# Layer 0's experts on one Trainium2 core: turning routes and vectors apart, and a new order for the opening and the rows

## The chip, the core and the metric

The kernel runs on one core of a Trainium2 chip (trn2). The metric is the device time of one execution in microseconds (us). The engines are PE (TensorE; its weight loads are shown as PEld), DVE (VectorE), ACT (ScalarE), POOL (GpSimd) and SP (SyncE, which here only issues transfers). "Line 1522" or "L1522" is a line of the kernel before; where a line of the changed kernel is meant, the text says so.

## What is computed

The reference is a stack of four layers, each a cross-attention and a feed-forward part with a layernorm ahead of both, on x of shape (4, 256, 256), four batches of 256 tokens, and a context of (4, 512, 128). Only layer 0 is touched. Its attention has 16 heads of 16 channels, with normed queries and keys, and its feed-forward part routes each token to 4 of 64 "arrows" (experts) of rank 16:

```python
vecs = jnp.einsum('arh,bsh->bsar', A, x)          # 64 arrows x 16 numbers for each token
arrows = jnp.linalg.norm(vecs, axis=-1)
_, idx = jax.lax.top_k(arrows, 4)
routes = jax.nn.one_hot(idx, 64).sum(-2) / 4      # 1/4 at the four chosen, else 0
v = jnp.einsum('bsa,bsar->bsr', routes, vecs)     # 16 numbers for each token
delta = jnp.einsum('bsa,ajr,bsr->bsj', routes, B, v)
return jnp.einsum('bsh,jh->bsj', x, W) + bias + delta
```

So `delta` is a product of u = routes x v, 64 x 16 = 1024 numbers for each token, with B as a matrix of 1024 x 256.

## The kernel before

All of layer 0 is written in an order fixed by hand for PE, ACT, DVE and POOL: each engine executes its instructions in the order in which the code records them, and waits at the head of its queue. SP's order is left to a scheduler. The code has these parts, in time:

- **The opening** (to about 21 us): loads, then for batch 0 the layernorm, queries, keys and values. `warm(n)` (line 1465) does n matmuls of the identity with itself, whose result nobody reads. `rows_of_biases` lets POOL build three selecting rows; `spread_biases` (line 1188) has PE spread three bias rows over 128 partitions and ACT copy them to `bqk`, which DVE then adds to queries (line 1219) and keys (line 1235). `ones_of_values` is a series of small POOL operations, `root_aside` (lines 1293 to 1296) a POOL root for the queries' norm.
- **The attention**, batch by batch, 8 steps a batch (4 groups of heads x 2 halves of the keys). In step i of batch b, PE does scores (line 1401), ACT their exponential (1405), PE the values of the group before (1411, 1420), DVE that group's `quotient`. `between(b, i)` (line 1613) fills in other work at each step: the next batch's preparation, `output0` of the batch before, and in the last batch's steps the norms (`Norm`, `layernorm_T`) of the experts' rows and the first chunk's `vectors` and `routes`.
- **The experts' stage** (137.5 to 220.5 us): 8 chunks of 128 tokens, two for each batch, one object of class `Arrows` (line 1471) each. Its methods: `vectors`: PE multiplies tokens with A (4 matmuls of 512 columns, line 1485), ACT writes squares and copies into a tile `two` (lines 1493, 1494). `routes`: DVE alone sums squares (1502), takes the best four (1504 to 1509), multiplies (1511) and sums to v (1513); then POOL makes u = route x v (1514), tokens on the partitions. `turned`: PE turns u in eight transposes of 128 x 128 (1522), ACT copies them to `uT` (1525). `output`: PE multiplies tokens with W (1531), adds `uT` times B (1535, 16 records), DVE adds the bias (1537), POOL adds to x (1538).
- Beside the chunks, **`folding`** (line 1003) is a generator that prepares layer 1: each step is 8 records on PE (1014), two more (1030), ACT and DVE copies. Its raw weights come over SP (`load_raw`, line 998). The loop at the end of the stage interleaves these by tables of counts; each chunk's `routes` stands two chunks ahead of its `turned`.

`layernorm_T` (line 939) turns a batch's tokens by four transposes on PE and one ACT copy. `layernorm_aside` (line 969) does the same with two DVE transposes of 32 x 32 blocks and sixteen small transfers on SP's queue. `Norm` needs a root on POOL (line 928) in the middle.

Of the kernel before, what the change touches and what calls it, by code (L numbers as in the profile page):

```python
# [17 lines left out]
P = 128  # L18
# [818 lines left out]
def bounded_path(ctx: ExitStack, tc: tile.TileContext, t, out: bass.AP, over):  # L837
# [34 lines left out]
    def load_c(b):  # L872
        (nc.sync if b else nc.scalar).dma_start(c_sb[:, b], t["ctx"][b].rearrange("(k p) c -> p k c", p=P))
# [181 lines left out]
    with tc.manual_schedule(engines={E.PE, E.Activation, E.DVE, E.Pool}):  # L1055
        c0 = ExitStack()
        l0 = c0.enter_context(tc.tile_pool(name="l0", bufs=1, side="right"))

        load_x(0)
        load_c(0)  # L1060
# [3 lines left out]
        wkv = l0.tile([P, 2, 2 * D], F32, tag="wkv", name="wkv")  # L1064
        nc.scalar.dma_start(wkv[:, 0, :], t["L0_wkv"])
# [3 lines left out]
        nc.scalar.preload_act_table_set("natural_log_exp_and_others")  # L1069

# [4 lines left out]
        rows1 = w0.tile([3, D + 3 * P], F32, tag="oT0", name="rows1")  # L1075
        crow = rows1[:, :D].rearrange("n (o d) -> n o d", o=1)
        takes = rows1[:, D:].rearrange("n (i p) -> n i p", p=P)


        brow = l0.tile([1, 2, 2 * D], F32, tag="brow", name="brow")  # L1080
        nc.sync.dma_start(crow[0:1, 0, :], t["L0_bq"].partition_broadcast(1))
        for i, n in enumerate(("L0_bkv", "L0_bdca")):
            nc.sync.dma_start(
                crow[1 + i : 2 + i, 0, :].rearrange("o (h x) -> o h x", x=HD0),
                t[n].rearrange("(o h x) -> o h x", o=1, x=2 * HD0)[:, :, :HD0],
            )
# [16 lines left out]
        wb = load_fw("wb", [P, 8, D], lambda w: [(w, t["F0_bT"].rearrange("(k p) n -> p k n", p=P))], "wb", f0w)  # L1103
# [10 lines left out]
        for i, n in enumerate(("qn", "kn", "knd")):  # L1114
            nc.gpsimd.dma_start(prm[:, i], t[f"L0_{n}"].partition_broadcast(P))
# [15 lines left out]
        nc.gpsimd.memset(c_last, 0.0)  # L1131
# [56 lines left out]
        def spread_biases():  # L1188
            pb = bank("mm", [P, 2, D], "pbias0")
            for i in range(2):  # L1190
                nc.tensor.matmul(pb[:, i, :], lhsT=takes[:, i, :], rhs=crow[:, 0, :], start=True, stop=True)
            pl = bank("mm", [P, D], "pbias1")
            nc.tensor.matmul(pl, lhsT=takes[:, 2, :], rhs=crow[:, 0, :], start=True, stop=True)
            nc.scalar.copy(bqk[:, 0:2, :], pb)
            nc.scalar.copy(bqk[:, 2, :], pl)
# [111 lines left out]
        def columns_of_norms():  # L1307
            wide = [P, 3, 2, HD0]
            by_lane = l0.tile(wide, F32, tag="by_lane", name="by_lane")
            pairs = l0.tile([P, 3, 2], F32, tag="pairs", name="pairs")  # L1310
            nc.vector.tensor_tensor(by_lane, prm, lane0[:, 0, None, None, :].to_broadcast(wide), ALU.mult)
            nc.vector.tensor_reduce(pairs, by_lane, AX.X, ALU.add)
            for o in range(2):
                nc.vector.tensor_scalar(
                    cols[:, o, :], pairs[:, 0, :], halves0[:, o : o + 1], HD0 ** -0.5, ALU.mult, ALU.mult
                )
            nc.vector.tensor_copy(cols[:, 2:, :], pairs[:, 1:, :])
# [152 lines left out]

        class Arrows:
# [24 lines left out]
            def routes(self):  # L1496
# [11 lines left out]
                route = small.tile([P, NA], F32, tag="route", name=f"route{u}")  # L1508
                nc.vector.tensor_scalar(route, rest[:, :NA], 0.0, 1.0 / TOPA, ALU.is_lt, ALU.mult)
                route_b = route[:, :, None].to_broadcast([P, NA, RA])  # L1510
                nc.vector.tensor_tensor(ar, ar, route_b, ALU.mult)
                v = small.tile([P, RA], F32, tag="v", name=f"v{u}")
                nc.vector.tensor_reduce(v, ar.rearrange("p a r -> p r a"), AX.X, ALU.add)
                nc.gpsimd.tensor_tensor(sq, route_b, v[:, None, :].to_broadcast([P, NA, RA]), ALU.mult)

            def turned(self):
                self.uT = w0.tile([P, 8, P], F32, tag="qT0", name=f"uT{self.u}")
                for n in range(2):
                    pt = bank("t", [P, 4, P], f"puT{self.u}_{n}")
                    for k in range(4):  # L1520
                        a0 = 8 * (4 * n + k)
                        nc.tensor.transpose(  # L1522
                            pt[:, k, :], self.two[:, 1, a0 : a0 + 8, :].rearrange("p a r -> p (a r)"), ident
                        )
                    nc.scalar.copy(self.uT[:, 4 * n : 4 * n + 4, :], pt)
# [15 lines left out]
        warm(9)  # L1541
        context_T(0)
        norm = Norm(0, "a0_0")
        rows_of_biases()
        last_context(0)
        mq = head_sums(by_head(wq0))
        xn = norm.tokens()
        warm(3)
        xnTs[0] = layernorm_T(xn, "a0_0")
        centred(by_head(wq0), by_head(wq0), mq)  # L1550
        centred(by_head(crow), by_head(crow), head_sums(by_head(crow), 3), 3)
# [6 lines left out]
        columns_of_norms()  # L1558
        warm(3)
        add_q = project_q(0)  # L1560
        spread_biases()
        add_q()
# [49 lines left out]

        def between(b, i):

            n = b + 1
            if n == 1:
# [76 lines left out]
            if b == B - 1:  # L1693
                if i in (0, 2, 6):
                    norms["f", i // 2] = Norm(min(i // 2, 2), f"f0_{min(i // 2, 2)}")
                if i in (1, 3, 7):
                    xns["f", i // 2] = norms["f", i // 2].tokens()
                if i in (3, 5):
                    k = (i - 3) // 2
                    xnTs["f", k] = layernorm_T(xns["f", k], f"f0_{k}")  # L1700
                if i == 4:
                    arrows[0] = Arrows(0)
                    arrows[0].vectors()
                if i == 5:
                    arrows[0].routes()
# [25 lines left out]
        arrows[1].routes()  # L1731
        arrows[0].turned()
        arrows[0].output()
        output0(B - 1)
# [14 lines left out]
        for n in range(B * NC):  # L1749
            if n + 2 < B * NC:  # L1750
                arrows[n + 2].routes()
            if n:
                arrows[n].turned()
            if n % NC == 0:
                if n + 3 < B * NC:
                    arrows[n + 3] = Arrows(n + 3)
                    arrows[n + 3].vectors()
                for _ in range((0, 0, 1, 1, 2, 2, 1, 1)[n]):
                    next(fold)
                if n == 6:  # L1760
                    xn1 = norm.tokens()
                if n:
                    arrows[n].output()
            else:
                k = n // NC + 2
                if k < B:
                    xnTs["f", k] = layernorm_T(xns["f", k + (k == 2)], f"f0_{k}")
                if n == 7:
                    first_xnT = layernorm_T(xn1, "a1_0")
                    next(fold)  # L1770
# [1709 lines left out]
```

## Time and profile before

| what | us |
|---|---|
| median of 3 runs | 1380.93 (1380.93 to 1382.0) |
| the profiled execution | 1380.97 |
| its span, first to last instruction | 1379.2 |
| first scores of batch 0 | 21.03 |
| last attention matmul of layer 0 ends | 137.46 |
| layer 1's first matmul starts | 220.46 |
| mean granted clock of TensorE | 0.999 |

The page gives the busy time of each engine, then the chain of work that ended last: followed back from the last instruction, at each step to what released it. Each row of the chain is a start, a length, an engine, a tile and a line; the number after x counts records (a matmul of this kernel leaves two, a transpose one), so rows are compared by their length. In the order of time, a bracket at a row's end gives how long the engine was idle before it and who released it. A busy PE in this profile is not PE at its peak, since matmuls' ends are modelled; what counts for the bound is whether one piece begins where the last ended.

In the stage from 137.46 to 168.40 DVE was busy 27.56 of 30.94 us, in 168.40 to 193.10 it was 18.92 of 24.70, and in 193.10 to 220.50 it was 11.51 of 27.40. PE has no idle time in any of the three.

### The profile page before, as it was taken

The page shows a single profiled execution, that of the slowest core. Times are in us where ns is not written, and L with a number is a line of the kernel's source. Part 1 is how long each engine was busy: PE and PEld are TensorE (multiplying, and loading weights), DVE is VectorE, ACT ScalarE, POOL GpSimd, SP SyncE. Part 2 cuts the span into 40 slices and gives each one's busy share as a digit, 9 for nine tenths or more (in the row PEclk, how much of TensorE's full clock was granted, in tenths as well). Part 3 has the DMA queues.
Part 4 walks back from the last instruction along what each step waited for, and adds up shares of the span by engine and source line. Part 5 has one row for each costly group of instructions (what it writes and reads, how often), then busy time and mean ns, then how long its engine had stood idle before and what let it go on. Part 6 is the DMA issues. An engine that isn't in the chain of part 4 may idle for free.

```text
span 1379.2 us, 20227 instructions
## 1 busy us (share of the span) xinstructions
PE 1369.2 (99%) x7221; PEld 903.1 (65%) x7221; DVE 897.2 (65%) x2052; ACT 572.6 (42%) x1134; POOL 699.4 (51%) x848
## 2 busy tenths in 40 slices
PE   9999999999999999999999999999999999999997
PEld 7665676566656667887565666666975665666666
DVE  6767863666666557655676756558656758566675
ACT  5766454433343332256434333333364334333331
POOL 5223333566565445352577655566325676444660
PEclk9999999999999999999999999999999999999999
DMA  5000220300000001361120000000432000000001
GB/s 171 15 3 2 77 78 17 89 19 8 16 5 19 0 13 43 83 218 48 47 54 15 17 0 16 0 1 16 124 119 69 7 12 4 1 8 1 0 1 34
DMA packets 77907, 50.79 MB, mean 37 GB/s; under 512 B 40628, under 2 KB 72645, under 8 KB 77799
## 3 DMA queue, kind: packets, MB, share of 16 engines
q1 hardware_dynamic: 72262, 36.13, 9.6%
q0 software_dynamic: 4176, 12.24, 3.1%
q8 instruction: 59, 0.97, 0.3%
q10 hardware_dynamic: 1360, 1.05, 0.2%
q14 instruction: 50, 0.40, 0.1%
HBM read 38.78 MB, written 6.95 MB: 33 GB/s over the span
## 4 chain that ended last, share of the span: by engine, by line
PE 97%; POOL 2%; DVE 1%; issue 0%; ACT 0%; POOLq 0%; DVEq 0%
PE ps L1948 23%; PE po L1956 23%; PE paq L1918 6%; PE pao L1918 5%; PE pbq L1918 4%; PE pbo L1918 4%; PE ps L1401 3%; PE po L1411 2%; PE pyf L1535 2%; PE paf L1485 2%; PE pgu L2496 2%; PE pm L1014 2%; PE psh L2317 2%; PE py L2042 2%; PE pn L1030 1%; PE pb L2901 1%
## 5 line engine op out<-in xcount | busy, mean ns | idle before, releaser
L1967 POOL TENSOR_TENSOR half<-pT 128x1024 f32<-128x1024 f32 x93 | 218.4, 2349 | 282.8 <-ACT pT L1951 228.0
L1948 PE MATMUL ps<-qT,cT 128*128 128x512 f32 x768 | 345.6, 593 | 0.0
L1956 PE MATMUL po<-pT,c_sb 128*128 128x512 f32 x768 | 345.3, 592 | 0.0
L1951 ACT ACTIVATE pT<-ps,mbias 128x512 f32<-128x512 f32 x384 | 263.8, 687 | 164.0 <-PE ps L1948 147.3
L1956 PEld LDWEIGHTS po<-pT,c_sb 128*128 128x128 f32 x768 | 145.8, 190 | 183.2 <-issue 183.2
L1948 PEld LDWEIGHTS ps<-qT,cT 128*128 128x128 f32 x768 | 138.9, 190 | 138.4 <-issue 136.1
L1960 ACT COPY oT<-po 128x512 f32<-128x512 f32 x96 | 56.2, 586 | 265.2 <-PE po L1956 265.2
L2003 POOL TENSOR_TENSOR oT<-oT,wide 128x512 f32<-128x512 f32 x84 | 106.8, 1291 | 0.0
L1928 DVE TENSOR_TENSOR qT<-qT,paq 128x128 f32<-128x128 f32 x90 | 25.2, 280 | 87.1 <-ACT qT L1927 87.1
L1405 ACT ACTIVATE pT<-ps 128x512 f32<-128x512 f32 x128 | 66.0, 602 | 21.6 <-PE ps L1401 21.4
L1975 DVE TENSOR_TENSOR half<-half 128x512 f32<-128x512 f32 x96 | 71.9, 749 | 2.7 <-POOL half L1965 2.5
L1977 DVE STREAM_TRANSPOSE turned<-half 128x512 f32<-128x512 f32 x96 | 68.3, 711 | 6.3
L1918 PE MATMUL paq<-xnT_a,m_sb 128*128 128x128 f32 x360 | 71.3, 280 | 0.0
L1928 DVE TENSOR_TENSOR w<-w,pao 128x128 f32<-128x128 f32 x21 | 6.0, 285 | 99.2 <-ACT w L1927 99.2
L1918 PE MATMUL paq<-xx,m_x 128*128 128x128 f32 x360 | 69.6, 275 | 0.0
L1918 PEld LDWEIGHTS paq<-xnT_a,m_sb 128*128 128x128 f32 x360 | 57.5, 192 | 18.2 <-issue 9.2
L1981 DVE TENSOR_REDUCE sums<-turned 128x16 f32<-128x512 f32 x96 | 65.9, 686 | 3.3
L1918 PE MATMUL pao<-n_x,ox 128*128 128x128 f32 x336 | 65.0, 275 | 0.0
L1927 ACT COPY qT<-paq 128x128 f32<-128x128 f32 x90 | 23.9, 265 | 94.2 <-PE paq L1918 93.2
L1931 DVE TENSOR_TENSOR qT<-qT,pbq 128x384 f32<-128x384 f32 x90 | 49.8, 554 | 9.4
L1918 PEld LDWEIGHTS paq<-xx,m_x 128*128 128x128 f32 x360 | 54.7, 192 | 0.0
L2002 DVE STREAM_TRANSPOSE wide<-rz 128x512 f32<-128x512 f32 x84 | 54.4, 686 | 0.0
(504 smaller groups left out, 2553.9 us busy)
## 6 DMA issues: line engine op xcount, KB each, us to landing
wq<-in_L_wqT SPq DMA_DIRECT2D x8, 512.0 KB
wo<-in_L_wo SPq DMA_DIRECT2D x8, 512.0 KB
yd<-yr SPq DMA_DIRECT2D x20, 128.0 KB
xnT_a<-y_a SPq DMA_DIRECT2D x144, 16.0 KB
xd<-xn_f SPq DMA_DIRECT2D x8, 256.0 KB
w<-in_F_w SPq DMA_DIRECT2D x4, 512.0 KB
wq<-in_L_wqT POOLq DMA_DIRECT2D x3, 512.0 KB
wo<-in_L_wo POOLq DMA_DIRECT2D x3, 512.0 KB
```

Source lines behind the costliest of these rows:

```text
L1405: nc.scalar.activation(pT[kp][:, j], ps[j], AF.Exp)
L1918: nc.tensor.matmul(p[:, at, :], lhsT=lhsT, rhs=rhs, start=(k == 0 and at == 0), stop=(k == len(of) - 1 and i == which[-1]),)
L1948: nc.tensor.matmul(ps, lhsT=cT[:, b, k * P : (k + 1) * P], rhs=qT, start=True, stop=True)
L1951: nc.scalar.activation(pT[:, k, :], ps, AF.Exp, bias=mbias[:, b, k : k + 1])
L1956: nc.tensor.matmul(po, lhsT=c_sb[:, b, k, :], rhs=pT[:, k], start=(k == 0), stop=(k == NK - 1))
L1960: done["head"] = nc.scalar.copy(raw, po).ins
L1967: nc.gpsimd.tensor_tensor(half, pT[:, 0:2], pT[:, 2:4], ALU.add)
L1975: nc.vector.tensor_tensor(part, half[:, 0], half[:, 1], ALU.add)
L1977: nc.vector.transpose(turned.rearrange("p f i -> p (f i)"), part)
L1981: nc.vector.tensor_reduce(sums[b, hp // 4][:, hp % 4, :], turned, AX.X, ALU.add)
L2002: nc.vector.transpose(wide, rzs[b, hp // 4][:, hp % 4, :, None].to_broadcast([P, NB, 32]))
L2003: eng.tensor_tensor(outs[b, hp], outs[b, hp], wide.rearrange("p f i -> p (f i)"), ALU.mult)
```

## The change

**The experts.** `routes` no longer makes u on POOL. It writes the routes twice side by side (64 + 64 columns) and keeps v. `turned` turns routes (128 x 128) and v (128 x 16) by one PE transpose each, writes the turned v to a scratch in DRAM (8 KB, issued by ACT), and loads it back by two transfers on SP's queue, each of 64 partitions, in which a row of v is repeated for all arrows (256 KB each). A new method `spread` multiplies this by the turned routes on POOL, in place; `uT` now lives in the tile `two`, which is held until `output`. The rows of B are loaded in another order to match (two transfers, 8 KB rows).

**Rows.** The tokens of batches 0, 1 and 2 for the experts are turned by `layernorm_aside`, batch 0's during the attention of batch 2, the others in the last batch's. Chunk 0 has `vectors` at step 2 of the last batch instead of 4, `routes` at 3 instead of 5, and now `turned` at 5 and `spread` at 6.

**The stage's order** is written out. `routes` of chunks 5, 6 and 7 come later than before against the outputs: that of chunk 7 is between `output(5)` and one step of the fold, followed by `turned(7)`. The norm of layer 1's first rows comes ahead of `output(6)`.

**The opening.** The bias rows are loaded first, on ACT's queue; context 0 moves from ACT's queue to SP's; three small parameter loads move from POOL's queue to ACT's; the biases are spread ahead of tokens, context and queries; the `warm` matmuls of its first part go from 9, 3 and 3 to 10.

The core of the diff:

```diff
@@ opening, loads
         load_x(0)
-        load_c(0)
-        wq0 = l0.tile([P, ND, D], F32, tag="wq0", name="wq0")
-        nc.sync.dma_start(wq0, t["L0_wq"].rearrange("(d p) n -> p d n", p=P))
...
-        nc.sync.dma_start(crow[0:1, 0, :], t["L0_bq"].partition_broadcast(1))
+        nc.scalar.dma_start(crow[0:1, 0, :], t["L0_bq"].partition_broadcast(1))
...
+        wkv = l0.tile([P, 2, 2 * D], F32, tag="wkv", name="wkv")
+        load_c(0)
+        nc.scalar.dma_start(wkv[:, 0, :], t["L0_wkv"])
+        nc.scalar.dma_start(wkv[:, 1, :], t["L0_wdca"])
...
+        for i, n in enumerate(("qn", "kn", "knd")):
+            nc.scalar.dma_start(prm[:, i], t[f"L0_{n}"].partition_broadcast(P))
@@ class Arrows, routes
-                nc.gpsimd.tensor_tensor(sq, route_b, v[:, None, :].to_broadcast([P, NA, RA]), ALU.mult)
+                self.route = sq.rearrange("p a r -> p (a r)")[:, : 2 * NA].rearrange("p (h a) -> p h a", h=2)
+                nc.vector.tensor_scalar(
+                    self.route, rest[:, None, :NA].to_broadcast([P, 2, NA]), 0.0, 1.0 / TOPA, ALU.is_lt, ALU.mult
+                )
+                nc.vector.tensor_tensor(ar, ar, self.route[:, 0, :, None].to_broadcast([P, NA, RA]), ALU.mult)
+                self.v = small.tile([P, RA], F32, tag="v", name=f"v{u}")
+                nc.vector.tensor_reduce(self.v, ar.rearrange("p a r -> p r a"), AX.X, ALU.add)
             def turned(self):
-                self.uT = w0.tile([P, 8, P], F32, tag="qT0", name=f"uT{self.u}")
-                for n in range(2):
-                    pt = bank("t", [P, 4, P], f"puT{self.u}_{n}")
-                    for k in range(4):
...
-                    nc.scalar.copy(self.uT[:, 4 * n : 4 * n + 4, :], pt)
+                two = self.two.rearrange("p n a r -> p n (a r)")
+                self.routeT, vT = two[:, 0, :P], two[:RA, 0, P : 2 * P]
+                self.uT = two[:, 1].rearrange("p (k s) -> p k s", s=P)
+                pt = bank("t", [P, 2, P], f"prT{self.u}")
+                nc.tensor.transpose(pt[:RA, 1, :], self.v, ident)
+                nc.tensor.transpose(pt[:, 0, :], self.route.rearrange("p h a -> p (h a)"), ident)
+                nc.scalar.copy(vT, pt[:RA, 1, :])
+                put = turned_v[:, (self.b * NC + self.c) * P : (self.b * NC + self.c + 1) * P]
+                nc.scalar.dma_start(put, vT)
+                nc.scalar.copy(self.routeT, pt[:, 0, :])
+                for h in range(2):
+                    nc.sync.dma_start(
+                        self.uT[64 * h : 64 * h + 64],
+                        put[8 * h : 8 * h + 8].rearrange("(o k) s -> o k s", o=1).to_broadcast([64, 8, P]),
+                    )
+            def spread(self):
+                nc.gpsimd.tensor_tensor(
+                    self.uT, self.uT, self.routeT[:, None, :].to_broadcast([P, 8, P]), ALU.mult
+                )
@@ opening, order
-        warm(9)
+        warm(10)
+        rows_of_biases()
+        norm = Norm(0, "a0_0")
+        nc.gpsimd.memset(c_last, 0.0)
+        centred(by_head(crow), by_head(crow), head_sums(by_head(crow), 3), 3)
+        spread_biases(0, 2)()
+        xn = norm.tokens()
+        xnTs[0] = layernorm_T(xn, "a0_0")
+        bias_last = spread_biases(2, 3)
         context_T(0)
...
         last_context(0)
...
@@ between(b, i)
+            if b == B - 2:
+                if i == 2:
+                    norms["f"] = Norm(0, "f0_0")
+                elif i == 3:
+                    rows_of_arrows(0)
...
+                if i in (0, 6):
+                    norms["f"] = Norm(1 + i // 6, f"f0_{1 + i // 6}")
+                if i in (1, 7):
+                    rows_of_arrows(1 + i // 6)
+                if i == 2:
                     arrows[0] = Arrows(0)
                     arrows[0].vectors()
+                if i == 3:
+                    arrows[0].routes()
                 if i == 5:
-                    arrows[0].routes()
+                    arrows[0].turned()
+                if i == 6:
+                    arrows[0].spread()
@@ the stage (after the last attention)
         for n in (1, 2):
             arrows[n] = Arrows(n)
             arrows[n].vectors()
-        arrows[1].routes()
-        arrows[0].turned()
+            arrows[n].routes()
         arrows[0].output()
+        arrows[1].turned()
         output0(B - 1)
...
+        def output(n):
+            arrows[n].spread()
+            arrows[n].output()
...
+        vectors(3)
+        norm = Norm(3, "f0_3")
+        vectors(4)
+        arrows[3].routes()
+        xn3 = norm.tokens()
+        arrows[2].turned()
+        output(1)
+        next(fold)
+        arrows[3].turned()
+        arrows[4].routes()
+        vectors(5)
+        output(2)
+        context_squares(0)
+        arrows[4].turned()
+        next(fold)
+        xnTs["f", 3] = layernorm_T(xn3, "f0_3")
+        arrows[5].routes()
+        output(3)
+        context_squares(1)
+        vectors(6)
+        arrows[5].turned()
+        next(fold)
+        output(4)
+        context_squares(2)
+        vectors(7)
+        arrows[6].routes()
+        next(fold)
+        arrows[6].turned()
+        output(5)
+        context_squares(3)
+        arrows[7].routes()
+        next(fold)
+        arrows[7].turned()
+        norm = Norm(0, "a1_0")
+        next(fold)
+        xn1 = norm.tokens()
+        output(6)
+        next(fold)
+        first_xnT = layernorm_T(xn1, "a1_0")
+        next(fold)
+        output(7)
         next(fold, None)
```

## The prediction

> **What bounds the kernel.** I read three views in this order: the page, the chain of work that ended last, and the order of time of DVE and POOL around that chain. From the page, the busy line and the chain's shares:
>
> ```profile
> PE 1369.2 (99%) x7221; PEld 903.1 (65%) x7221; DVE 897.2 (65%) x2052; ACT 572.6 (42%) x1134; POOL 699.4 (51%) x848
> ...
> PE 97%; POOL 2%; DVE 1%; issue 0%; ACT 0%; POOLq 0%; DVEq 0%
> ```
>
> TensorE is the bound, so time leaves only where PE does less or stops waiting, and time comes back wherever the new order makes PE wait. The experts' stage runs from 137.46 us (end of the last attention matmul) to 220.46 us (first matmul of layer 1). The chain view shows it closed, piece on piece, all PE:
>
> ```profile
> 185.31 0.87 PE puTf L1522 x8
> 186.19 3.44 PE paf L1485 x8
> ...
> 198.32 0.86 PE pyf L1531 x4
> 199.18 3.45 PE pyf L1535 x16
> 202.63 0.89 PE pm L1014 x8
> 203.53 0.86 PE pn L1030 x2
> ...
> 213.96 0.44 PE pxn_a L945 x4
> ```
>
> Each piece begins where the one before ends. So here is the price list: eight transposes of a chunk 0.87 us, four of a layernorm 0.44, `vectors` 3.44, one step of the fold 0.89 + 0.86 = 1.75, `output` 0.86 + 3.45 = 4.31. DVE, in order of time around chunk 7:
>
> ```profile
> 197.55 0.42 DVE L1537 TENSOR_TENSOR ysf<-pyf,bias 128x256 f32<-128x256 f32 x1 [3.70 <-PE pyf L1535]
> 197.91 1.21 DVE L1502 TENSOR_REDUCE nrf<-twof 128x64 f32<-128x1024 f32 x1
> ...
> 201.44 1.90 DVE L1513 TENSOR_REDUCE vf<-twof 128x16 f32<-128x1024 f32 x1
> ```
>
> `routes` lasts from 197.91 to 203.34: 5.43 us, longer than an `output`. In the kernel before, this was two chunks ahead of its use (chunk 7's transposes came at 213.08), so nothing waited. This is the number on which the forecast turns.
>
> **What goes.** (1) A chunk's `turned` falls from eight transposes to two (routes, vectors): 0.87 x 2/8 = 0.22, so 0.65 less; eight chunks, **-5.2**. (2) The rows of batches 0, 1, 2 are turned by DVE and DMA (`layernorm_aside`) instead of PE: 3 x 0.44 = **-1.3**. Each takes sixteen small loads on SP's queue. SP issued sixteen of the same kind (L967) in 10.9 us (59.90 to 70.71); batch 2's start about 2 us after the attention's end and are needed 15 us after it, behind three `vectors` and an `output`. The loads of chunk 1's `uT` stand behind them on SP, about level with their data.
>
> (3) The opening. The biases' matmuls (10.79 to 12.28 on the chain, three pieces) stood between the queries' and the keys' matmuls; now they come first, so DVE's addition of the first keys could start at about 11.9 instead of 13.38. But POOL's queue caps this:
>
> ```profile
> 14.34 0.29 POOL L1168 COPY vals_d<-rows 128x128 f32<-128x128 f32 x1
> ...
> 16.45 0.25 POOL L1296 TENSOR_TENSOR hr<-hr,he 128x32 f32<-128x32 f32 x1
> ```
>
> POOL was busy without a gap from 9.24 to 14.63; its root ended at 16.70, 0.34 before DVE's scaling used it at 17.04. The copies of the last context now wait for a copy that ACT does after the tokens' one: 0.4 to 0.5 later than 8.88. So the root ends near 16.3 and scaling starts near 16.35: -0.7. Against it: ACT now issues three small loads, and in the built program the last of them waits until the second context load has landed, with the biases' copy queued behind it, and behind that the tokens' copy, the context's copy, POOL. That load starts right behind three of 256 KB; x was issued at 0.80 and first used at 3.92, and DMA moved about 200 GB/s between 5 and 15 us. Four such loads beside two on the other queue end between 6.5 and 9 us, and each us past 7.5 costs one. I take **-0.6**; ends -1.9 and +1.5. The removed `warm` matmuls stood in waits. The nine at the start took 4.21 us, 0.47 each, three at 8.12 only 0.67, 0.22 each: TensorE was at half speed until about 7. The ten now reach to about 6.2, where the biases' matmuls follow if their three small loads, now first on ACT's queue, land by 5.3; so the rise isn't put off. The two-part load of `wb` (same bytes, first used after 146 us) and POOL's moved memset are hidden.
>
> Sum of what goes: -5.2 - 1.3 - 0.6 = **-7.1**.
>
> **What comes.** Dropped from `routes`, POOL's product (L1514, 1.93 us) returns as `spread`, a POOL operation of the same 128x1024 shape behind the DMA round trip; no row shows this form, the nearest are L1514, 1.93, and L1967, 2.35 at the same width. I take 2.0. The new waits of PE, each by the order of the built program:
>
> (a) Chunk 0, `turned` in the last attention's sixth eighth. After the values of the fourth eighth, DVE has a quotient (120.23 to 122.70: 2.5), `quad` (1.1), then `routes`, 5.4, plus about 0.2 of handing over: 9.2. PE meanwhile has scores and values of two eighths (1.07 + 1.00 + 1.08 + 1.00 + 0.43) and two `output0` halves (0.86 to 1.06 each): 6.5. PE waits **2.7**, with scores queued behind. The `vectors` that used to fill this (3.43 at 123.01) moved two eighths earlier.
>
> (b) `output(1)`: its `spread` stands on POOL behind the root of batch 3's norm, which waits for DVE, which first does both `routes` of chunks 1 and 2, three additions and the statistics. From the end of the attention: 3.4 + 0.6 + 2 x 5.4 + about 3.2 + 0.8 + 2.0 = 20.8; PE arrives after 2 x 3.44 + 4.31 + 0.22 + 1.75 + 2 x 3.44 + 0.22 + 0.86 = 21.1. Level; POOL's additions delay the statistics, I take **0.8** (0 to 1.2).
>
> (c) `output(3)`: `spread(3)` follows the addition of `output(2)`: 0.4 + 0.75 + 2.0 + 0.3 = 3.45 after it; PE has 0.22 + 1.75 + 0.44 + 0.86 = 3.27. **0.2** to 0.5; 0.3.
>
> (d) Chunk 6: `routes(6)` stands on DVE behind the addition of `output(4)`: 0.1 + 0.4 + 5.4 + 0.1 = 6.0; PE has one `vectors` and one fold step, 5.19. **1.0** with `spread(5)` on POOL beside it.
>
> (e) Chunk 7: `routes(7)` stands behind the addition of `output(5)`: again 6.0; PE has one fold step, 1.75. PE waits **4.25**. This is the largest term, and no buffer or transfer can shorten it.
>
> (f) `output(6)`: the norm of layer 1 now precedes it, so POOL's root waits for the statistics behind `routes(7)`, and `spread(6)` waits behind the root though its data came long before. After `routes(7)`: copy 0.63 + statistics 1.37 + root 0.08 + 0.70 + spread 2.0 + 0.1 = 4.9. PE: 0.1 + 0.22 + 1.75 + 0.86 = 2.95. **1.95**.
>
> (g) The DVE turning inside attention (norm, tokens, two transposes of about 0.4 each per batch, one set moved into batch 2) delays quotients there, where PE's banks wait for them: **0.8**; 0 to 1.5.
>
> Sum of what comes: 2.7 + 0.8 + 0.3 + 1.0 + 4.25 + 1.95 + 0.8 = **11.8**. Net 11.8 - 7.1 = **+4.7**. The profiled execution took 1380.97 (span 1379.2 and 1.8 around it); the median of the runs is 1380.93. Forecast: **1385.7**.
>
> The round trip itself (a write of 8 KB, then two loads of 256 KB) has no row. I bound a hop by nothing and by x's load, 3.1 us, so both by 0 to 6.2, and take 5, near x. SP's queue adds: a load can stand behind the fold's weights (for chunk 4, one 512 KB load that waits for PE's `pm`). PE reaches `output(n)` 8 us or more after `turned(n)` for most chunks, and POOL is held longer by (b) to (f), so at up to about twice the price it is covered; beyond that chunks 1, 2 and 3 pay, 1 to 2 us each.
>
> [...] In this trace a DVE TENSOR_SCALAR of two columns (L927) took 983 ns instead of 170 where POOL's L1514 ran beside it. [...]
>
> **Rivals.** *The round trip decides*: if write and loads together take over 8 us, at chunks 1 to 3, 5 and 7 `spread` starts when the data land. Against it: no transfer of this trace alone took that long. Price 1 to 2 us at five places: about +7 more, 1393. *DVE is not late at the end* (the other side): chunks 6 and 7 arrive in time and POOL's root with them, so (d), (e), (f), 7.2 us, fall away; with an opening at its good end (1.3 more) the sum is 11.8 - 7.2 - 7.1 - 1.3 = -3.8: 1377.2. It decides if `routes` takes under 1.7 us behind an addition; its reductions alone are 1.21 and 1.90. *Nothing to measure*: the opening at its good end, (b), (c), (g) at nought, (a) at 2: -1.3 - 0.8 - 0.3 - 0.8 - 0.7 = -3.9 off the forecast, 1381.8.
>
> **Numbers.** Forecast case 0.62 (1383.8 to 1390), nothing to measure 0.18, round trip 0.12, DVE in time 0.08. Its own bounds: -3.9 as above, and +2.1 (opening), +0.7 (g), +0.8 (b, spread at 2.35), +2 (ports): 1381.8 to 1391.3. The range 1380.5 to 1392 leaves out 0.08 below and a good half of the round trip. A measurement of this kernel can tell 0.2%, 2.8 us, from no change. Slower by more: 0.62 + 0.12 = 0.74; within: 0.18; faster: 0.08.
>
> **What would show it.** The stage from the last attention matmul to layer 1's first holds 11.8 - 2.7 - 0.8 = 8.3 us of PE gaps; the longest, 4 us, ahead of chunk 7's transposes with DVE's `v` as releaser; the next ahead of the second part of `output(6)`, released by POOL; one of 2 to 3 us ahead of chunk 0's transposes. The first scores start near 20.4 instead of 21.03. It is wrong if those gaps are missing, if `spread` is released by a DMA, or if the first scores start after 22.

## The result, and the profile after

The changed kernel takes **1400.9 us** (median of 4 runs, 1397.86 to 1401.59); the kernel before, run beside it, 1381.47 (4 runs, 1380.93 to 1382.21). The ratio is 1.0135, 95% interval 1.0123 to 1.0148: slower by 19.4 us. The forecast was 1385.7, its range ended at 1392: the sign was right, the size a quarter of what came (+4.7 against +19.5 between the two profiled executions).

The profiled execution of the changed kernel took 1400.46, its span is 1398.7, its mean granted clock 0.991 (0.999 before). From its page, the busy line and the chain's shares:

```profile
PE 1372.2 (98%) x7151; PEld 901.4 (64%) x7151; DVE 903.6 (65%) x2058; ACT 566.3 (40%) x1131; POOL 699.6 (50%) x845
...
PE 93%; POOL 2%; DVE 2%; DMA 2%; issue 0%; ACT 0%; SPq 0%; ACTq 0%; DVEq 0%; POOLq 0%
```

TensorE has 70 fewer records and yet is busy for 3.0 us more, and DMA stands on a chain that held none before. The first says that the same matmuls became slower, the second that a transfer decides somewhere. The stage where both happen is found by three times, all read from the order of time of PE:

| us | before | after |
|---|---|---|
| first scores | 20.96 | 23.18 |
| from there to the end of the last attention matmul | 116.49 | 119.69 |
| from there to layer 1's first matmul (the stage) | 82.85 | 99.00 |
| the rest | 1158.9 | 1156.8 |

The rest isn't touched by the change; it varied between 1156.8 and 1160.4 from one profiled run of the changed code's variants to another. Part of that is the clock: e12 has no stretch at half clock up to the end of the stage, and its mean granted clock is still 0.997, an estimated 8 us at half later on (1377 x 0.003 x 2; 0.999 before). So +2.2 opening, +3.2 attention, **+16.15 stage**.

In the stage, PE in the order of time (start, length, tile and line; the bracket is the idle time before, and who ended it):

```profile
169.11 5.30 PE L1549 MATMUL pyf<-wb,twof 128*128 128x256 f32 x16 [4.95 <-POOL twof L1537]
...
180.97 3.72 PE L1549 MATMUL pyf<-wb,twof 128*128 128x256 f32 x16 [0.30 <-POOL twof L1537]
...
191.85 5.41 PE L1549 MATMUL pyf<-wb,twof 128*128 128x256 f32 x16 [3.88 <-POOL twof L1537]
...
224.45 0.37 PE L1524 MATMUL prTf<-ident,vf 128*16 128x128 f32 x1 [4.28 <-DVE vf L1517]
...
224.83 1.91 PE L1014 MATMUL pm<-wk,wq 128*128 128x128 f32 x8
```

The first three are the second part of `output(1)`, `(2)` and `(3)`, the fourth chunk 7's transposes. Two things are to be seen. There are three waits of about 4 to 5 us, where the forecast had one of them. And after each long wait the work itself is slow: the same sixteen matmuls take 5.3 to 5.4 us behind a long wait and 3.72 behind a short one; the fold's `pm` takes 1.91 where it usually takes 1.05. POOL's rows name what `output` waited for:

```profile
166.72 2.34 POOL L1537 TENSOR_TENSOR twof<-twof 128x1024 f32<-128x1024 f32 x1 [4.40 <-DMA twof<-turned_v]
...
178.57 2.35 POOL L1537 TENSOR_TENSOR twof<-twof 128x1024 f32<-128x1024 f32 x1 [2.90 <-DMA twof<-turned_v]
...
189.46 2.34 POOL L1537 TENSOR_TENSOR twof<-twof 128x1024 f32<-128x1024 f32 x1 [3.50 <-DMA twof<-turned_v]
```

Each of these three is released by the DMA that loads the spread vectors. The chain of waits gives that round trip for chunk 3 piece by piece:

```profile
177.04 2.88 DMA turned_v<-twof
...
180.67 8.62 DMA twof<-turned_v
...
189.46 2.35 POOL twof L1537
...
191.85 5.41 PE pyf L1549 x16
```

From 177.04, where ACT issues the write of 8 KB, to 189.30, where the loads have landed, are **12.3 us** (2.9 the write, 9.4 from there to the end of the loads). Chunk 1 took 11.7 us, chunk 5 10.2. The slow work shows in the clock column. Busy time by engine in two stretches of after (stretch, its length, five engines' busy time, then the granted clock, the DMA share and GB/s):

```profile
169.00:172.00 3.00, 2.89 (x7) 2.35 (x8) 0.53 (x2) 0.00 (x0) 0.06 (x1) 0.50 0.77 237
...
223.75:230.00 6.25, 5.55 (x17) 4.17 (x18) 3.67 (x10) 2.02 (x7) 3.05 (x2) 0.50 0.29 54
```

The clock is 0.50 right behind the waits. Read in steps of 0.25 us it was half in after from 8.49 to 15.32, 134.78 to 138.20, 168.92 to 172.34, 192.81 to 196.22 and 223.53 to 230.36, and nowhere in this part of the kernel before. Every such stretch is 3.41 us long or twice that, and their starts lie whole multiples of 3.41 apart (134.78 is 8.49 + 37 x 3.413). The column doesn't show the slow start: in the kernel before it reads 1.00 from the first microsecond, where nine `warm` take 0.47 us each instead of 0.22. That is read from the matmuls' own lengths.

**Theory R:** the round trip is 10 to 14 us and decides at `output(1)` to `(5)`, and the clock lost behind each long wait is paid on top. **Rival D:** DVE's late `routes`, as the forecast had it, are most of the loss. **For the opening, A:** ACT is held by the third parameter load; **B:** TensorE ran out of `warm` work and lost the clock.

### The profile page after: what moved, and what is told of

The parts are those of the page before. It is cut to its first block, busy times and chain, and to the rows that moved or that the text cites. A ratio compares the mean times of both kernels' runs of the same rounds, so it can differ in the third digit from the quotient of the medians.

```text
span 1398.7 us, 20219 instructions
## 1 busy us (share of the span) xinstructions
PE 1372.2 (98%) x7151; PEld 901.4 (64%) x7151; DVE 903.6 (65%) x2058; ACT 566.3 (40%) x1131; POOL 699.6 (50%) x845
## 3 DMA queue, kind: packets, MB, share of 16 engines
q1 hardware_dynamic: 87204, 41.37, 11.7%
## 4 chain that ended last, share of the span: by engine, by line
PE 93%; POOL 2%; DVE 2%; DMA 2%; issue 0%; ACT 0%; SPq 0%; ACTq 0%; DVEq 0%; POOLq 0%
PE ps L1986 23%; PE po L1994 23%; PE paq L1956 6%; PE pao L1956 5%; PE pbq L1956 4%; PE pbo L1956 4%; PE ps L1402 3%; PE pyf L1549 2%; PE po L1412 2%; PE pgu L2534 2%; PE psh L2355 1%; PE py L2080 1%; PE pm L1014 1%; PE pn L1030 1%; DMA twof<-turned_v 1%; PE paf L1488 1%
```

## The experiments

All ratios are to the kernel before, run on the same chip. "Stage" is the time from the end of the last attention matmul to layer 1's first matmul, in the profiled run: 82.85 before, 99.00 after.

| run | us | ratio, 95% interval | attention | stage |
|---|---|---|---|---|
| e1 no transfers | 1390.74 | 1.0066 (1.0049-1.0083) | 119.77 | 86.75 |
| e2 rows of 4 KB | 1393.29 | 1.0095 (1.0078-1.0111) | 119.69 | 89.90 |
| e3 filled waits | 1405.45 | 1.0172 (1.0151-1.0193) | 119.76 | 102.93 |
| e4 routes(7) early | 1403.89 | 1.0162 (1.0145-1.0179) | 119.70 | 101.31 |
| e5 parameters on POOL | 1405.91 | 1.0173 (1.0156-1.0190) | 119.70 | 99.22 |
| e6 warm 15 | 1401.35 | 1.0143 (1.0126-1.0160) | 120.99 | 98.97 |
| e7 4 KB and routes(7) early | 1391.16 | 1.0067 (1.0047-1.0086) | 120.96 | 87.08 |
| e8 re-ordered | 1388.72 | 1.0044 (1.0028-1.0061) | 115.33 | 89.26 |
| e9 paced | 1382.29 | 1.0010 (1.0001-1.0019) | 115.32 | 83.69 |
| e10 paced, 512 bytes | 1405.94 | 1.0177 (1.0162-1.0193) | 115.32 | 107.47 |
| e11 spread in halves | 1378.50 | 0.9983 (0.9970-0.9995) | 115.33 | 80.79 |
| e12 parameters on SP | 1377.59 | 0.9967 (0.9955-0.9979) | 115.33 | 80.28 |

### e1: without the round trip

```diff
 put = turned_v[...]
-nc.scalar.dma_start(put, vT)
 nc.scalar.copy(self.routeT, pt[:, 0, :])
-for h in range(2):
-    nc.sync.dma_start(self.uT[64 * h : 64 * h + 64], put[8 * h : 8 * h + 8]...)
```

> Leaves out the write of the turned v to DRAM and both loads back; spread multiplies what already lies in the tile, so delta is not the reference's. All instructions of PE, DVE, POOL and the rest of ACT stay in their order. Theory R (the round trip of the transfers sets the waits ahead of the second part of output(1) and output(3)): the wait of 4.95 us falls to about 1, that of 3.88 to about 0.5, the small ones of 0.3 and 0.4 go, and with them the half clock behind the two long ones (about 3.5 us): 11 us less than the changed kernel, near 1390; the wait of 4.3 us ahead of chunk 7's transposes stays. Theory Q (the order on POOL and DVE sets them, as predicted): less than 1.5 us gained, 1399 to 1401.

Measured 1390.74, as R expected. What PE waited for in the stage (total us, times, longest):

```profile
PE prTf L1524 <- DVE vf L1517: 6.2, 2, 4.3
PE pyf L1543 <- POOL twof L1531: 1.0, 3, 0.4
```

The transfers are worth 12.25 us of the stage, clock included. Of what D had forecast, the waits at chunks 6 and 7 are here, 1.94 and 4.28 us, but not the one at `output(6)`; it is the smaller part. R stands.

### e2: the same bytes in rows of 4 KB

The scratch holds a chunk's v as 16 rows in a piece, so that one partition's eight rows are 4 KB in a piece instead of eight of 512 bytes.

```diff
-turned_v = dram0.tile([RA, B * NC * P], ...)
+turned_v = dram0.tile([B * NC, RA, P], ...)
-put = turned_v[:, (self.b * NC + self.c) * P : (self.b * NC + self.c + 1) * P]
+put = turned_v[self.b * NC + self.c]
-    self.uT[64 * h : 64 * h + 64],
-    put[8 * h : 8 * h + 8].rearrange("(o k) s -> o k s", o=1).to_broadcast([64, 8, P]),
+    two[64 * h : 64 * h + 64, 1],
+    put[8 * h : 8 * h + 8].rearrange("(o k) s -> o (k s)", o=1).to_broadcast([64, 8 * P]),
```

> The scratch is laid out by chunks, so that a partition's 8 rows are one piece of 4 KB instead of eight of 512 bytes; bytes, transfers and order stay. If the number of pieces sets the loads' 9 us (1024 pieces of 512 bytes), the loads fall to 3 to 4 us and the time comes within 2 us of the run without transfers: 1389 to 1392. If the bytes or the fixed cost set them, the time stays near 1400.

Measured 1393.29, 1.3 past the expected 1389 to 1392, but nowhere near 1400: 9.1 of e1's 12.25 us of stage come back with no byte less. The chain of e2 around chunk 2:

```profile
164.12 5.52 DMA turned_v<-twof
...
170.21 4.42 DMA twof<-turned_v
...
177.20 3.72 PE pyf L1549 x16
```

The loads take 4.4 instead of 8.6 to 9.5 us. Of the round trip the write is now the longer half: 5.5 us for 8 KB, while the fold's weights are on their way, against 1.44 for chunk 1's write in after. The remaining waits in the stage were 1.19, 2.09, 0.36, and the same 1.93 and 4.28 by DVE.

### e3: the waits filled with idle matmuls

If the clock is lost because PE waits, `warm` matmuls in the wait should keep it.

```diff
+FILLS = {"f0_1": 21, "f0_3": 16}     # ahead of the second part of output(1), output(3)
+if self.u in FILLS: warm(FILLS[self.u])
...
+warm(18)
 arrows[7].turned()
```

> Dummy matmuls of the identity (0.21 us each at full speed) fill the three long waits of the stage: 21 ahead of the second part of output(1), 16 of output(3), 18 ahead of chunk 7's transposes. Theory C (a long wait is paid twice, since the clock is granted at half for one or two windows of 3.4 us after it): the waits stay, the granted clock stays at 1.00, and about 6.5 us go (1.7 + 1.8 + 3.0): near 1394. If the slow matmuls after the waits have another cause: no gain, 1400 to 1402.

Measured 1405.45, slower than after: a miss. The clock did stay at 1.00 through the three filled waits, and the loss reappeared at the two outputs that hadn't waited that long:

```profile
182.44 5.41 PE L1553 MATMUL pyf<-wb,twof 128*128 128x256 f32 x16 [1.94 <-POOL twof L1539]
...
231.59 6.66 PE L1553 MATMUL pyf<-wb,twof 128*128 128x256 f32 x16 [2.97 <-POOL twof L1539]
```

So the two parts of R don't add. Behind `turned(n)` a round trip runs at its own pace; while PE works at half clock, that time is cover. A PE that keeps its clock arrives earlier and waits for much the same landing: `spread(2)` starts at 179.52 against 178.57 in after, `spread(3)` at 189.60 against 189.46. At these places of after, a chunk's serial path (turned, write, loads, `spread`, `output`) is the bound, not PE. Why e3 came out slower than after, and not level with it, is not settled.

### e4: routes(7) ahead of output(5)

```diff
 arrows[6].turned()
+arrows[7].routes()
 output(5)
 context_squares(3)
-arrows[7].routes()
```

> Only routes of chunk 7 is moved, from behind output(5) to ahead of it. If routes on DVE behind the addition of output(5) is what chunk 7's transposes wait for: the wait of 4.3 us and the 3 us of half clock behind it go, and output(6) then waits some 2.7 us for spread(6), which stands behind POOL's root: 3 to 4.6 us less, 1396 to 1398. If output(6) has no wait: 1393.5. If the cause is another: no change.

Measured 1403.89 with the wait for chunk 7's v gone: a miss. The longest wait of all stands one output later, PE first and POOL's `spread(6)` second:

```profile
231.62 5.59 PE L1549 MATMUL pyf<-wb,twof 128*128 128x256 f32 x16 [7.29 <-POOL twof L1537]
```

```profile
229.23 2.34 POOL L1537 TENSOR_TENSOR twof<-twof 128x1024 f32<-128x1024 f32 x1 [4.94 <-DMA twof<-turned_v]
```

Chunk 6's write left at 215.15 and landed at 219.44, behind four of the fold's weight loads, the vectors landed at 229 (14 us in all). The 4.28 us of (e) had been hiding this.

### e5 and e6: the opening

e5 puts the three parameter loads back on POOL's queue; e6 leaves them and gives PE five more `warm` matmuls.

```diff
 e5:
-    nc.scalar.dma_start(prm[:, i], ...)        # on ACT's queue
+    nc.gpsimd.dma_start(prm[:, i], ...)        # behind POOL's first memsets
 e6:
-warm(10)
+warm(15)
```

> The changed kernel with the three small parameter loads back on POOL's queue, right behind its first memsets. In the traces so far the third of them holds ACT until context 1 has landed (8.6 to 9.5 us), and the copies of biases, tokens and context stand behind it; the first scores start at 23.0 to 24.3 instead of 20.96. Theory A (ACT's queue): the tokens' copy goes from 9.4 to 10.3 down to about 8.5, the queries' matmuls start near 9, the first scores at 21.4 to 22, 1.5 to 2.5 us less in all (1398 to 1399); the half clock from 8.5 to 15.3 stays, since the 1 us wait of PE ahead of the biases' matmuls stays. Theory B (the half clock alone delays the opening): no change of the first scores.

> The changed kernel with 15 instead of 10 warm matmuls at the start, so that PE works until about 6.8 us, when the biases' rows are ready. Theory B: the clock stays at 1.00 from 8.5 to 15.3, and the queries' matmuls take 2.0 instead of 3.6 us; if the clock alone is late, the first scores come 1.9 us earlier (near 21.2). Theory A: queries still start behind ACT's copy at 10 or later, and DVE's first addition stands behind the operation that waits for the third parameter load (13.2): 0.4 us earlier at most.

In after, the ten `warm` end at 5.70 and the bias rows are ready 1.06 us later; then the clock is half from 8.49. That wait in after, then the queries of batch 0 in after and in e6 (PE, order of time; before had 1.99 for them, from 8.80):

```profile
6.77 1.10 PE L1191 MATMUL pbias<-rows 3*128 3x256 f32 x4 [1.06 <-DVE rows L1180]
```

```profile
10.36 3.62 PE L1209 MATMUL pq<-wq,xnT_a 128*128 128x256 f32 x8
```

```profile
9.79 1.99 PE L1209 MATMUL pq<-wq,xnT_a 128*128 128x256 f32 x8
```

In e6 that wait is filled, the clock stays up through the opening, and the first scores start at 20.76 instead of 23.18, as B expected. e5 missed: the bias rows landed only near 8.1 us, PE waited 3.61 us for them, the clock was half from 8.05 to 18.3, and the first scores came at 26.59. Why those rows, still first on ACT's queue, landed 2.4 us later was not settled. In after ACT's copy of the biases started at 8.96 behind the third load (issued 8.58), as the forecast's step says.

Other profiles show that B is not the whole. With 10 `warm` the first scores start at 22.84 to 24.30 in seven profiles; with the 15 of e6 they start at 21.59 in e9 and 20.80 in e10, but at 23.49 in e11. There the third load is issued at 9.74 (8.28 in e6), the queries wait for ACT's copy of the tokens, and the clock is half from 10.96 to 14.37:

```profile
11.24 3.52 PE L1209 MATMUL pq<-wq,xnT_a 128*128 128x256 f32 x8 [0.39 <-ACT xnT_a L948]
```

In e1, e4 and e7 too, a wait of 1.2 to 1.6 us ahead of the queries is for this copy, and half clock sets in during it. So A's hold can go together with B's loss. In e8 (10 `warm`) the slow start itself lasts longer: the bias matmuls at 6.39 take 2.04 us, the queries 3.20, and the first scores come at 23.53. How the 2.2 us of after divide between A and B is not settled.

But e6's total is that of after. Its 2.4 us went again: chunk 0's wait in the attention cost two stretches at half clock instead of one (131.07 to 137.9; attention 120.99), and the rest of the layers took 2.4 us more than in after's profile, within the spread given above.

### e7: 4 KB and routes(7) early

e2's edit and e4's together.

> Both the scratch by chunks (4 KB pieces) and routes of chunk 7 ahead of output(5). Theory R: with the short round trip the wait that came instead of chunk 7's (7.3 us ahead of output(6) in the run with the move alone) is mostly gone; what is left there, 2 to 2.7 us, is the order on POOL, where spread(6) stands behind the root of layer 1's first norm. Against the run with 4 KB pieces alone: minus 4.3 and minus 1.7 of half clock, plus 2.3 and up to 1.7: 1390 to 1391.5. If the round trip is not the cause of that 7.3 us wait: no better than 1394.

Measured 1391.16, as expected. Moving `routes(7)` now pays in the stage (89.90 to 87.08), since the transfer behind it is short; what is left at the end is the forecast's term (f), `spread(6)` behind the norm's root:

```profile
217.37 5.41 PE L1549 MATMUL pyf<-wb,twof 128*128 128x256 f32 x16 [2.32 <-POOL twof L1537]
```

### e8 and e9: an order that keeps each wait off PE

e8 takes e7 and re-orders: chunk 0 is turned behind the last attention matmul, batch 2's rows by PE, `spread(1)` and `spread(6)` ahead of the norms' roots, one step of the fold earlier.

```diff
 i == 3: -arrows[0].routes()        i == 5: +arrows[0].routes()  (was turned)
 values(*before, po, range(NK), True)
+arrows[0].turned(); arrows[0].spread()
 quotient(*before[:2], po, oTs[B - 1])
...
+xnTs["f", 2] = layernorm_T(xns["f", 2], "f0_2")
 arrows[0].output()
-arrows[1].turned()
 output0(B - 1)
+arrows[1].turned(); arrows[2].routes()
...
+arrows[1].spread()
 norm = Norm(3, "f0_3")
...
+next(fold)
 arrows[6].turned()
+arrows[7].routes()
 output(5)
...
+arrows[6].spread()
 norm = Norm(0, "a1_0")
```

> A version built on the theory that three things cost the time: the round trip (scratch by chunks, 4 KB pieces), DVE's order (routes of chunk 0 in the last attention's sixth eighth as before, routes of chunk 7 ahead of output(5), those of chunk 2 behind the last output0), and what stands ahead of spread on POOL and SP (spread of chunks 0, 1 and 6 ahead of the quotient's additions and the norms; rows of batch 2 turned by PE; one fold step moved ahead of chunk 6's transposes). The opening is left as in the changed kernel. If the theory holds: the stage from the last attention matmul to layer 1's first falls from 99.0 to 80 to 83 us (before: 83.0), from the first scores to the last attention matmul to about 117 (before 116.4, changed 119.6), and the time is that of before plus the opening's 2 to 3 us: 1380 to 1384. If something else costs the time: above 1386.

Measured 1388.72; half of it held. The attention is at 115.33, 1.16 less than before: without chunk 0 in it, the removed transposes show, and no loss (g) is left. The stage was 89.26 instead of 80 to 83, because `output(1)` and `output(6)` still waited 2.77 and 2.00 us: their write and loads ran beside the fold's weights. e9 moves those, and its two other edits give chunk 6 more room:

```diff
-warm(10)
+warm(15)
+load_raw(1, 0, arrows[1].last.ins)   # the fold's first weights behind chunk 1's loads
+arrows[6].routes()
 output(4)
...
-arrows[6].routes()
-next(fold); next(fold)
 arrows[6].turned()
 arrows[7].routes()
+next(fold)
...
 arrows[6].output()
+next(fold)
```

> The reordered version once more, with two things that its trace asks for and with 15 warm matmuls. There the waits of 2.8 us ahead of output(1) (and 3.1 us of half clock behind it) and of 2.0 us ahead of output(6) come from fold weights that are issued just before a chunk's transfers and slow them. Now the first fold weights follow chunk 1's loads, and chunk 6 is turned ahead of the fold step that frees the buffers for the last weights (its routes ahead of output(4)). If the theory holds: first scores at 20.7 to 21.2, from there to the last attention matmul 115.3, from there to layer 1's first matmul 79 to 82 us (before: 82.9): layer 1 starts at 215 to 218 instead of 220.3, and the time is 2 to 5 us under that of before, 1376 to 1380. If something else holds the stage: not below that of before.

Measured 1382.29 (11 runs): 2.3 us above the expected range's end, and level with the kernel before; the stage, 83.69, missed 79 to 82 as well. In the profile no stretch at half clock is left up to the end of the stage. What PE waited for there:

```profile
PE pyf L1549 <- POOL twof L1537: 4.3, 4, 1.3
PE prTf L1524 <- DVE vf L1517: 0.4, 1, 0.4
```

### e10: the pieces again, alone, in e9's order

e9 with the scratch and the loads as in after (e2's edit undone). This is one difference only, in the best order so far.

> The same version with the scratch as in the changed kernel, so that the loads come in 1024 pieces of 512 bytes. Theory R: each round trip is some 5 us longer, in an order that gives a chunk 8 to 9 us from its transposes to the second part of its output: waits of 2 to 5 us at chunks 0, 1, 2, 3 and 6 and half clock behind the longer ones, 15 to 25 us more than with 4 KB pieces: 1393 to 1403. If the order alone decides: within 3 us of the version with 4 KB pieces.

Measured 1405.94, 23.65 more than e9, within the 15 to 25 of Theory R. Chain pieces of e10 for chunk 3:

```profile
179.62 3.76 DMA turned_v<-twof
...
184.14 8.90 DMA twof<-turned_v
...
193.20 2.63 POOL twof L1537
```

The stage grows by 23.8 us (107.47 against 83.69), with six waits of PE for `spread`, 20.2 us in all, and the clock lost behind four of them. The layout also changes where the write puts its rows; the write and the loads weren't tried apart.

### e11 and e12: two small steps past it

e11: `spread` as two POOL operations of 128x512, so that PE starts with the first half. e12: also the three parameter loads on SP's queue instead of ACT's.

```diff
 e11:
-nc.gpsimd.tensor_tensor(self.uT, self.uT, self.routeT[:, None, :]..., ALU.mult)
+for k in (0, 4):
+    half = self.uT[:, k : k + 4, :]
+    nc.gpsimd.tensor_tensor(half, half, self.routeT[:, None, :]..., ALU.mult)
 e12:
-nc.scalar.dma_start(prm[:, i], ...)
+nc.sync.dma_start(prm[:, i], ...)
```

> The paced version with spread in two POOL operations of 128x512, so that the first four of output's matmul pairs wait for half of it only. In the paced version the four waits left in the stage (0.9, 1.1, 1.3, 1.0 us, all released by POOL) are shorter than or about as long as half a spread (2.35 / 2 = 1.2). If what stands between the transfers and PE is spread's own length: those waits fall to 0.3 or less each, 3 to 4 us go, and the time is 1378 to 1379.5, under that of before (1381.8) by 0.15 to 0.3%. If POOL's fixed cost or another wait takes their place: 1381 to 1383.

> As the version with spread in halves, and the three small parameter loads on SP's queue, behind context 0, so that ACT waits for no landing before its copies and DVE's first sums of parameters don't wait for the third load (11.4 us in the run with 15 warm matmuls). Theory A (ACT's queue holds the opening, once the clock stays up): first scores near 20.0 instead of 20.8 to 21.6, 0.8 to 1.5 us less than the version with spread in halves. Theory B (the clock alone): the same first scores, the same time within 0.5 us.

e11: 1378.5, as expected, stage 80.79; of the four waits for `spread` one is left, 0.99 us, and one of 1.51 us for the fold's weights is new. e12: **1377.59** against 1381.89 of the kernel before (0.9967, 0.9955 to 0.9979): faster than both kernels. e12's intervals and e11's overlap, so the last step alone isn't shown. The first scores of e12 are at 20.89, not at 20.0 as expected (e11's 23.49 has the half clock shown above): ACT is no longer held, but POOL's queue caps the opening, as the forecast said. DVE's first work behind that root:

```profile
17.03 0.73 DVE L1296 TENSOR_TENSOR pad<-qk,hr 128x512 f32<-128x512 f32 x1 [0.50 <-POOL hr L1293]
```

## Why the prediction was right in sign and wrong in size

Against +4.7, the profiled executions differ by 19.5. By the prediction's own terms:

- **(a), (d), (e)**, DVE late for a transpose: forecast 2.7, 1.0, 4.25; measured 2.65, 0.88, 4.28. (a) and (e) were read from rows of the same queue, and they hold: reading DVE's queue in the order of time was the right method. (d) came out by luck. Its 1.0 was meant "with `spread(5)` on POOL beside it", which in after came only at 212.28, when the transfer let it; the wait of 0.88 is shown as ACT's, and DVE's v was ready 0.1 us before it ended. In e1, e2 and e7 `spread(5)` does run beside `routes(6)`, a DVE operation of 0.23 us takes 1.23 to 1.29, and the wait is 1.93, DVE's. That operation in e1, and `spread(5)` beside it:

```profile
198.69 1.23 DVE L1512 TENSOR_SCALAR twof<-restf 128x128 f32<-128x128 f32 x1
...
197.48 2.36 POOL L1531 TENSOR_TENSOR twof<-twof 128x1024 f32<-128x1024 f32 x1
```

- **(b), (c)**: forecast 0.8 + 0.3; measured 4.95 at `output(1)` and 3.88 at `output(3)`, with 0.30 and 0.40 at two others: 8.4 more in all. The cause was not POOL's root or an addition ahead of `spread` but the loads, as the prediction's own test ("if `spread` is released by a DMA") says.
- **(f)**: forecast 1.95, measured 0: PE, at half clock behind (e), took 5.5 us from chunk 7's transposes (224.45) to this part (229.95) instead of the 2.95 worked out, and `spread(6)` ended at 229.35. In e7 it is there, 2.3.
- **(g)**: forecast 0.8; e8's attention shows no such loss.
- **Clock**, in no term: 1.5 in the attention (136.19: 1.94 instead of 1.07; 134.45: 1.81 instead of 1.15), and about 6.4 in the stage (1.7, 1.8 and 2.9 behind the three long waits).
- **The opening**: forecast -0.6, measured +2.2. The step that failed is that the ten `warm` "reach to about 6.2, where the biases' matmuls follow": the ten took 4.17 us, as long as nine before (4.21), and ended at 5.70, while the last of the three loads landed at 5.68 instead of by 5.3 and DVE's two operations on the rows, which no term held, took until 6.66. The hold of ACT was as forecast.
- **The transposes**, by their rows (0.22 us a chunk instead of 0.87, and chunk 0's out of the stage): 5.4 of the stage, forecast 5.2. Three of the four row turnings left PE as forecast, one of them (0.44) from the stage. The sixteen loads from 59.90 to 70.71 took 10.8 us and not 10.9, which changes nothing.

The sum of these differences: +8.4 round trip, +7.9 clock, +2.8 opening, -0.8 (g), -1.95 (f), -0.1 (d), and -2.1 in layers that the change doesn't touch: 14.15 of the 14.8 by which the forecast was off. By the same sum the stage is 14.7 (waits) + 6.4 (clock) - 5.9 (transposes and rows) = 15.2 of 16.15. e3 warns against taking this sum as a list of independent prices: with the clock kept, the waits grew.

**The step that failed** is the price of the round trip: "bound a hop by nothing and by x's load, 3.1 us, so both by 0 to 6.2, and take 5, near x", covered "at up to about twice the price". x's load and this one have the same 256 KB a transfer, but these come in 512 pieces of 512 bytes. The two loads' 1024 pieces took about 9 us, and the same bytes in 128 pieces of 4 KB took 4.4 (e2), 4.1 in e9. The round trip measured 10.2 to 12.3 us instead of 5, and what it left uncovered cost 8.4 us more than forecast. The bound from above was no bound: the nearest row is no upper end for a shape that the trace doesn't hold. With it failed a term that the sum had at nothing, the half clock behind long waits: 7.9 us. The rival *round trip decides*, given 0.12, is what happened; it was worked out as +7 and was more, since at one or two us a place it held no wait of 5 and nothing for the clock.

**DVE beside POOL.** The row of 983 ns instead of 170 has its like in after. Two operations of DVE's `routes`, each beside a `spread` on POOL (178.57 and 189.46):

```profile
178.79 2.21 DVE L1512 TENSOR_SCALAR twof<-restf 128x128 f32<-128x128 f32 x1
...
189.63 3.25 DVE L1515 TENSOR_TENSOR twof<-twof 128x1024 f32<-128x1024 f32 x1
```

With POOL not in a `spread` these took 0.23 us (at 220.85) and 1.22 (at 181.11). PE's two long waits by DVE, (a) and (e), are as long as forecast without this, so in after it cost nothing to speak of; in e1, e2 and e7 it is 1.0 of the 1.93 us at chunk 6. No run shows the last +2 of the forecast's bounds as time of the kernel: an operation of DVE grew by 2.0 us, a wait of PE by 1.0.

**Waits and the clock.** In every run that has it, a wait of 2.65 us, shorter than one stretch of 3.41 us at half clock, went with one such stretch or two.

## What to carry to other kernels

Price a transfer by its pieces and by what is already on its way, not by its bytes (here 512 KB took about 9 us in pieces of 512 bytes and 4.4 in pieces of 4 KB, and a write of 8 KB took 1.44 to 5.5), and when no row has the same shape of pieces, give the bound no upper end from a row of another shape. In these traces a wait of TensorE of 2.65 us or more cost its own length and a stretch of 3.41 us or more at half clock; but where a transfer behind it was the real bound, filling the wait gained nothing (e3). Waits stand in series behind one another: taking a long one away (e4) showed the next, and only the pieces, the order and the weights' place together, and then `spread` in halves (e11, e12), made the change's saving of transposes visible, as 0.2 to 0.3% of the time.

## What the runs showed that was not expected

- In the attention and the stage, none of PE's waits up to 1.5 us was followed by half clock; of nine waits of 1.9 to 2.35 us in e1, e2, e3, e5, e7 and e8, two were; all of 2.65 us or more were. One wait was followed by one stretch of 3.41 us or by two (in e5's opening, after 3.61 us, by three). In the openings less went with it: 1.06 us in after, 0.39 us in e11. What decides between them for a given wait was not shown.
- A write of 8 KB took 1.44 us from issue to landing where little else ran (chunk 1 in after), and 4.3 (e4) and 5.5 us (e2) behind the fold's weights.
- In after, ACT's third parameter load, of 16 KB, was issued only at 8.58, right after context 1 had landed on SP's queue (8.56). So in this program a load held its engine until a transfer of another queue had landed.
